# Three expert slots taken from the count before the last two chunks, and multiplied behind the last chunk's routing

## The chip, the cores and the metric

The kernel runs on one core of a Trainium2 chip. The metric is the device time of one execution in microseconds (us); the time of a kernel is the median of its timed runs. The engines are TensorE (PE, with its weight loads as PEld), VectorE (DVE), ScalarE (ACT), GpSimd (POOL) and SyncE (SP), whose work here is to issue DMAs.

## The reference, cut to what matters

The whole computation is four layers over 3125 nodes of 256 values: an attention layer, a mixture of 16 experts with two experts for each node, a graph sum, and a mixture of 8 experts with one expert for each node. Only the last layer is touched by the change:

```python
def _L1_ffn_ref(x, W1, b1, Wg, bg, Wd, bd):          # C = 256, HID = 1024, E = 8
    H = gelu(x @ W1 + b1)
    probs = softmax(H @ Wg + bg)
    assign = argmax(probs)
    out = zeros_like(x)
    for e in range(8):
        y = H @ Wd[e] + bd[e]
        out = out + where(assign == e, probs[:, e:e + 1] * y, 0)
    return out
x = x + _L1_ffn_ref(_layernorm(x), ...)
```

Each node goes through a common hidden layer of 1024 values, picks one of 8 experts by the gate, and is multiplied with that expert's 1024 x 256 weights. The result is weighted by the gate's probability and added to the node's x.

## The kernel before, in words

The last layer is the function `routed_top1`. It works in two phases.

**Routing.** The nodes come in 25 tiles of 128, and these in chunks of four tiles (512 nodes): six full chunks and a seventh with one tile, of which 53 nodes are real. A loop over the chunks (line 895 on) does this for each:

- PE computes the hidden layer `H` in eight parts (line 901) and ACT applies the Gelu (line 903).
- PE multiplies `H` with the gate's weights (line 910, `ps_zT`). DVE takes the result out as `zs` (line 912). PE folds it into logits (line 915), and DVE finds each node's expert (`first_max`, lines 240 to 248, and `sel`, line 921).
- `pre` (line 924) adds up `sel` tile by tile. Two small products on PE (lines 925 and 926) make of `sel` and `pre` each node's rank among the nodes of its expert, and DVE turns this into `to`, the node's row in a buffer in HBM called `rows` (line 933). Each expert has its own area of `rows`, filled without gaps from its start.
- ACT computes the Exp for the probability (line 936). Exp and Gelu need different tables, which ACT loads in between.
- For each tile, PE transposes `H` back (line 945, `ps_rows`), ACT or DVE copies it into `row` (line 946), POOL copies x in beside it (line 947), and DVE adds the node's number and probability (lines 948 and 949). POOL then issues an indirect DMA that scatters the 128 rows of 1282 values into `rows` (line 950).

**Slots.** A slot is one full or partly filled tile of 128 rows of one expert. Behind the last chunk, PE sums the number of nodes of each expert (`ps_n`, line 956), and DVE computes from it a table of slots: for each the expert and the first row (lines 959 to 987). While that goes on, `keep_warm` (line 555) lets PE multiply zeros. Then 30 slots run (`slots`, line 1007 on). For each:

- SP reads expert and row from the table (lines 1009 and 1011), loads the 128 rows into `hs` (line 1015), and loads the expert's bias (line 1017). The first slot's load is split in two. The pool of `hs` has four buffers. Since `rows` is written by scatters with addresses known only at run time, a load waits for all scatters ahead of it.
- PE transposes the tile (line 1022, `ps_cols`) and ACT copies it into `hsT` (line 1023).
- PE multiplies it with the expert's weights, which stay in SBUF (line 995, `ps_y`). DVE adds the bias (line 998), computes the weighted sum `y` (line 999), and casts the nodes' numbers to `who` (line 1002). POOL scatters `y` to the output (line 1003). The multiplication of a slot is issued behind the transposes of the next.

Two more slots (30 and 31) stand behind a branch that is taken only if the table has more than 30 (`rest`, line 969).

A scheduler of the language orders the instructions of each engine and puts in the waits. It takes both from the tiles that instructions read and write, and from the memory that a tile takes over when a pool is closed and the next one opened. The pools of the routing phase (`uh` for H, `ur` for rows, and others) are closed before the pools of the slots (`vx` for `hs`, `bias` and `hsT`, and others) are opened.

Of the kernel before, what the change touches and what calls it, by code (L numbers as in the profile page):

```python
# [9 lines left out]
F32 = mybir.dt.float32  # L10
F16 = mybir.dt.float16
BF16 = mybir.dt.bfloat16
I32 = mybir.dt.int32
# [3 lines left out]
OP = mybir.AluOpType  # L17
AX = mybir.AxisListType
# [3 lines left out]
P = 128  # L22
N = 3125
NT = 25
LAST = N - (NT - 1) * P
NP = NT * P
D = 256
# [10 lines left out]
NX1, HID1 = 8, 1024  # L38
EPS = 1e-5
CHUNK = 512  # L40
# [484 lines left out]
SLOTS = (N + NX1 * (P - 1)) // P  # L525
USUAL = 30
ROW0 = D + 2
ROW1 = HID1 + D + 2
# [23 lines left out]
def keep_warm(nc, ps, held, rows, times):  # L552

    for _ in range(times):
        nc.tensor.matmul(ps, held, rows, start=True, stop=True)


def independent(tc, group, made):

    tc.declare_no_dep(made.ins, group=group, reason="rows of different tokens")  # L560
    tc.add_to_no_dep_group(group, made.ins)
# [295 lines left out]
def routed_top1(tc, x, xnT, ident, iota, count, weights, rows, out, over):  # L857
# [4 lines left out]

    nc = tc.nc
    before, every = count
    (a, b1, (g, fold), gb), (d, bd) = weights
    nh = HID1 // P
    with tc.tile_pool(name="u1", bufs=1) as cp:
# [9 lines left out]
                                channel_multiplier=-1)  # L877
# [6 lines left out]
        warm = cp.tile([P, P], F32, name="warm")  # L884
        nc.gpsimd.memset(warm, 0.0)
        rest = cp.tile([1, 1], I32, name="rest")
        end = cp.tile([1, 4, 2 * NX1], F32, name="end")
        nc.vector.memset(end, 0.0)
        with tc.tile_pool(name="uh", bufs=2) as hp, tc.tile_pool(name="uw", bufs=2) as wp, \
             tc.tile_pool(name="ur", bufs=6) as rp, \  # L890
# [4 lines left out]
            for c in range(0, NP, CHUNK):  # L895
                n = min(CHUNK, NP - c)
                H = hp.tile([P, nh, CHUNK], F32, name="H")
# [55 lines left out]


            total = pg.tile([1, NX1], F32, name="ps_n")
            nc.tensor.matmul(total, every[:, 0:1], pre[:, NT], start=True, stop=True)
            nc.scalar.copy(warm[0:1, :NX1], total)
            keep_warm(nc, tp.tile([P, CHUNK], F32, name="ps_rows"), warm, d[:, 0, 0:2].rearrange("p j f -> p (j f)"), 8)
# [4 lines left out]

            nc.vector.tensor_copy(end[:, 0, NX1:], ni)
            for j in range(3):
                nc.vector.tensor_tensor(end[:, j + 1, NX1:], end[:, j, NX1:], end[:, j, NX1 - (1 << j):-(1 << j)],
                                        op=OP.add)
            end = end[:, 3, NX1:]
            nc.vector.tensor_scalar(rest, end[:, NX1 - 1:], float(USUAL), None, op0=OP.is_gt)
            slot = cp.tile([1, SLOTS], F32, name="slot")  # L970
            nc.gpsimd.iota(slot, pattern=[[1, SLOTS]], base=0, channel_multiplier=0,
                           allow_small_or_imprecise_dtypes=True)
            done = cp.tile([1, SLOTS, NX1], F32, name="done")
            nc.vector.tensor_tensor(done, end[:, None, :].to_broadcast([1, SLOTS, NX1]),
                                    slot[:, :, None].to_broadcast([1, SLOTS, NX1]), op=OP.is_le)
            ex = cp.tile([1, SLOTS], F32, name="ex")
            nc.vector.tensor_reduce(ex, done, AX.X, OP.add)
            nc.vector.tensor_scalar(table[:, 0], ex, float(NX1 - 1), None, op0=OP.min)

            nc.vector.tensor_tensor(done, done, ni[:, None, :].to_broadcast([1, SLOTS, NX1]), op=OP.mult)  # L980
            skip = cp.tile([1, SLOTS], F32, name="skip")
            nc.vector.tensor_reduce(skip, done, AX.X, OP.add)
            nc.vector.tensor_tensor(slot, slot, skip, op=OP.subtract)
            nc.vector.tensor_scalar(ex, ex, float(NT), None, op0=OP.mult)
            nc.vector.tensor_tensor(slot, slot, ex, op=OP.add)

            nc.vector.tensor_scalar(table[:, 1], slot, float(NX1 * NT), float(P), op0=OP.min, op1=OP.mult)

        def slots(which, pools):
            xp, sp, tp, po = pools  # L990

            def multiply(hs, hsT, bias, e):
                ps = po.tile([P, D], F32, name="ps_y")
                for j in range(nh):
                    nc.tensor.matmul(ps, hsT[:, j], d[:, ds(e, 1), j, :].rearrange("p o f -> p (o f)"),  # L995
                                     start=(j == 0), stop=(j == nh - 1))
                y = sp.tile([P, D], F32, name="y")
                nc.vector.tensor_tensor(bias, ps, bias, op=OP.add)  # L998
                nc.vector.scalar_tensor_tensor(y, bias, hs[:, HID1 + D + 1:], hs[:, HID1:HID1 + D], op0=OP.mult,  # L999
                                               op1=OP.add)  # L1000
                who = sp.tile([P, 1], I32, name="who")
                nc.vector.tensor_copy(who, hs[:, HID1 + D:HID1 + D + 1])  # L1002
                independent(tc, "out", nc.gpsimd.indirect_dma_start(  # L1003
                    out=out, out_offset=bass.IndirectOffsetOnAxis(ap=who, axis=0), in_=y, in_offset=None,
                    bounds_check=N - 1, oob_is_err=False))

            ready = None
            for s in which:
                e = nc.values_load(table[0:1, 0, s:s + 1], engines=(mybir.EngineType.PE, mybir.EngineType.SP), min_val=0,  # L1009
                                   max_val=NX1 - 1, skip_runtime_bounds_check_because="min with the last expert")  # L1010
                at = nc.values_load(table[0:1, 1, s:s + 1], engines=(mybir.EngineType.SP,), min_val=0,  # L1011
                                    max_val=NX1 * NP, skip_runtime_bounds_check_because="min with the spare tile")
                hs = xp.tile([P, ROW1], F32, name="hs")
                for c, n in ((0, ROW1),) if s else ((0, HID1 // 2), (HID1 // 2, ROW1 - HID1 // 2)):
                    nc.sync.dma_start(hs[:, c:c + n], rows[ds(at, P), c:c + n])  # L1015
                bias = xp.tile([P, D], F32, name="bias")
                nc.sync.dma_start(bias, bd[ds(e, 1), :].to_broadcast([P, D]))  # L1017
                hsT = xp.tile([P, nh, P], F32, name="hsT")
                for h in range(0, nh, 4):
                    ps = tp.tile([P, 4, P], F32, name="ps_cols")  # L1020
                    for j in range(4):
                        nc.tensor.transpose(ps[:, j], hs[:, (h + j) * P:(h + j + 1) * P], ident)  # L1022
                    nc.scalar.copy(hsT[:, h:h + 4], ps)  # L1023
                if ready:
                    multiply(*ready)
                ready = hs, hsT, bias, e
            multiply(*ready)

        def pools(stack, bufs):
            return [stack.enter_context(tc.tile_pool(name=name, bufs=b, **kw)) for name, b, kw in (  # L1030
                ("vx", min(4, bufs), {}), ("vs", bufs, {}), ("vpt", min(4, bufs), dict(space=PSUM)),
                ("vpo", min(3, bufs), dict(space=PSUM)))]

        with ExitStack() as stack:
            slots(range(USUAL), pools(stack, 6))
# [719 lines left out]
```

## Time and profile before

| | |
|---|---|
| Time of the kernel (median of 3 runs) | 1934.22 us (1934.16 to 1934.34) |
| The profiled execution: its own time | 1933.04 us |
| The profiled execution: span from first to last instruction | 1931.3 us |
| Mean granted PE clock | 0.991 of full |
| PE busy, DVE busy, ACT busy, POOL busy | 97%, 52%, 39%, 15% of the span |
| ps_y multiplications of the slots (line 995) | 480, 108.8 us busy |
| ps_H multiplications of the routing (line 901) | 224, 93.1 us busy |
| Last full chunk's zs copied out (line 912) | at 1766.37 us |
| Last chunk's scatter of rows issued (line 950) | at 1782.96 us |
| First load of a slot issued (line 1015) | at 1786.94 us |
| First transposes of a slot (line 1022) | at 1791.57 us |

Times within the profile are microseconds from the start of the span. An fp32 multiplication is recorded as two passes, so that eight products of a slot count as 16. Matmuls are pipelined, so two groups that follow one another may overlap a little in the records. The granted clock is the share of full speed that the chip allowed PE in a stretch of time.

### The profile page before, as it was taken

The numbers are of one execution on the slowest core, as the hardware profiler recorded it, in microseconds if no ns is written. First come the engines' busy times: TensorE is split into PE (matmuls) and PEld (weight loads), VectorE is DVE, ScalarE is ACT, GpSimd is POOL, SyncE is SP. The second block draws the span as 40 slices with busy tenths as digits, with TensorE's granted clock in tenths as the row PEclk, the third lists the DMA queues.
The fourth block names the chain that finished last, engine by engine and source line by source line (L and its number), as shares of the span: only waits on it lengthen the run. The fifth ranks groups of instructions, "written<-read, shape, count | busy, mean of one in ns | idle before, by whom it ended". The sixth has DMA issues, their size and how long they took to land. (4 is left out here: it accounts for less than half of the span.)

```text
span 1931.3 us, 27975 instructions
## 1 busy us (share of the span) xinstructions
PE 1867.0 (97%) x9466; PEld 1482.0 (77%) x9466; DVE 1002.7 (52%) x2909; ACT 748.3 (39%) x2254; POOL 297.2 (15%) x454
## 2 busy tenths in 40 slices
PE   6999999999999999999999989999989999999998
PEld 4788888887788888788888757777668887455887
DVE  6889888785555555567777722222235222334122
ACT  4767777672000011122222221111127999544221
POOL 4200000000000000022333222233320000132122
PEclk9999999999999999999999989999999999999999
DMA  4101123475100000021111165657540000633664
GB/s 124 32 10 64 40 67 121 198 288 231 68 1 1 1 1 3 9 56 45 44 45 44 39 201 145 193 175 235 128 107 2 1 1 1 229 137 143 214 209 138
DMA packets 103577, 182.96 MB, mean 95 GB/s; under 512 B 10054, under 2 KB 72741, under 8 KB 103392
## 3 DMA queue, kind: packets, MB, share of 16 engines
q1 hardware_dynamic: 72268, 124.32, 18.9%
q0 software_dynamic: 16016, 34.28, 6.5%
q10 hardware_dynamic: 15138, 22.44, 3.6%
q8 instruction: 80, 1.31, 0.3%
q14 instruction: 75, 0.61, 0.1%
HBM read 92.93 MB, written 90.17 MB: 95 GB/s over the span
## 5 line engine op out<-in xcount | busy, mean ns | idle before, releaser
L1263 PE MATMUL acc<-big,pm 128*128 128x257 f32 (+1 forms) x3750 | 872.1, 383 | 5.2 <-DVE pm L1260 4.8
L1263 PEld LDWEIGHTS acc<-big,pm 128*128 128x128 f32 (+1 forms) x3750 | 681.3, 187 | 111.4 <-DVE pm L1260 10.3
L1260 DVE SCALAR_TENSOR_TENSOR pm<-tau,rho,counts 128x256 f32<-128x256 f32 (+1 forms) x975 | 437.0, 467 | 160.3 <-PE acc L1263 157.5
L762 PE MATMUL ps_h<-xsT,w 128*128 128x384 f32 x512 | 167.8, 486 | 0.5 <-ACT xsT L738 0.5
L1382 PE MATMUL acc<-msg,cr 128*128 128x512 f32 (+1 forms) x625 | 157.9, 403 | 0.0
L1594 DVE TENSOR_TENSOR ohk<-iota_k,key 128x1200 f16<-128x1200 f16 x196 | 151.7, 775 | 5.7 <-PE acc_c L1606 5.4
L762 PEld LDWEIGHTS ps_h<-xsT,w 128*128 128x128 f32 x512 | 97.2, 190 | 65.1 <-ACT xsT L738 0.7
L1382 PEld LDWEIGHTS acc<-msg,cr 128*128 128x128 f32 (+1 forms) x625 | 114.7, 185 | 29.2 <-ACT cr L1378 1.2
L1378 ACT ACTIVATE cr<-counts 128x256 fp32r<-128x256 uint8 (+1 forms) x325 | 130.5, 402 | 14.6 <-PE acc L1382 7.0
L1606 PE MATMUL acc_c<-ohk,ohs 128*128 128x200 f16 x1176 | 130.6, 250 | 0.6 <-ACT ohs L1591 0.6
L1590 ACT ACTIVATE far<-iota_s,low 128x128 f16<-128x128 f16 x360 | 123.4, 397 | 6.1 <-POOL far L1588 1.8
L1606 PEld LDWEIGHTS <-ohs 128*128 128x128 f16 x1176 | 105.3, 98 | 25.9 <-ACT ohs L1591 1.0
L995 PE MATMUL ps_y<-t_wd,hsT 128*128 x480 | 108.8, 380 | 0.4 <-ACT hsT L1023 0.4
L765 ACT ACTIVATE silu<-ps_h 128x384 f32<-128x384 f32 x64 | 31.4, 490 | 199.6 <-PE ps_h L762 199.6
L766 DVE TENSOR_TENSOR hid<-silu,ps_h 128x384 f32<-128x384 f32 x64 | 35.5, 554 | 136.9 <-PE ps_h L762 134.5
L1609 ACT CAST counts<-acc_c 128x400 uint8<-128x400 f32 x196 | 93.0, 479 | 34.7 <-PE acc_c L1606 34.0
L995 PEld LDWEIGHTS ps_y<-t_wd,hsT 128*128 128x128 f32 x480 | 88.8, 190 | 11.6 <-ACT hsT L1023 0.6
L1243 ACT ACTIVATE tau<-ps_m 128x256 f32<-128x256 f32 (+1 forms) x39 | 14.1, 369 | 215.5 <-PE ps_m L1241 197.3
L780 POOL DMA_INDIRECT sums<-y,who x48 | 74.9, 1561 | 128.1 <-DVE y L778 118.5
L901 PE MATMUL ps_H<-big,t_w 128*128 128x512 f32 (+1 forms) x224 | 93.1, 552 | 0.8 <-ACT H L903 0.5
L775 PE MATMUL ps_o<-w,hid 128*128 128x256 f32 x384 | 86.8, 379 | 0.0
L1594 DVE TENSOR_TENSOR ohs<-iota_s,low 128x512 f16<-128x512 f16 (+1 forms) x196 | 83.6, 427 | 0.0
(298 smaller groups left out, 1933.2 us busy)
## 6 DMA issues: line engine op xcount, KB each, us to landing
rows<-empty SPq DMA_DIRECT2D x16, 2564.0 KB, 15.1
w<-in_L_ffn_w_dram ACTq DMA_DIRECT2D x42, 512.0 KB, 7.6
hs<-rows SPq DMA_DIRECT2D x29, 641.0 KB, 4.2
w<-in_L_ffn_w_dram SPq DMA_DIRECT2D x30, 512.0 KB, 5.3
rows<-empty SPq DMA_DIRECT2D x16, 516.0 KB, 4.3
t_wd<-in_L_ffn_Wd_dram SPq DMA_DIRECT2D x8, 1024.0 KB, 12.5
xs<-rows SPq DMA_DIRECT2D x15, 387.0 KB, 5.5
bias<-in_L_ffn_bd_dram SPq DMA_DIRECT2D x30, 128.0 KB
```

Of the source, the lines that this page charges most:

```text
L762: nc.tensor.matmul(ps, w[:, k, j * P:(j + 1) * P], xsT[:, k], start=(k == 0), stop=(k == KD - 1))
L775: nc.tensor.matmul(ps, hid[:, j, q * P:(q + 1) * P], o[:, j], start=(j == 0), stop=(j == nh - 1))
L901: nc.tensor.matmul(ps[:, :n], a[:, k, j * P:(j + 1) * P], xnT[:, k, c:c + n], start=(k == 0), stop=(k == KD - 1))
L995: nc.tensor.matmul(ps, hsT[:, j], d[:, ds(e, 1), j, :].rearrange("p o f -> p (o f)"), start=(j == 0), stop=(j == nh - 1))
L1260: nc.vector.scalar_tensor_tensor(pm[:, :n], tau[:, :n], now.rho[:, s:s + 1], edges[:, s, :n], op0=OP.max, op1=OP.mult)
L1263: nc.tensor.matmul(acc[:r, j, :D + 1], pm[:, q:q + r], now.h[:, s], start=(s == 0), stop=(s == NT - 1))
L1378: nc.scalar.activation(cr[:, :n], edges[:, s, :n], AF.Copy, accum_out=seen[:, a * NT + s:a * NT + s + 1])
L1382: nc.tensor.matmul(acc[:r, j].rearrange("p h d -> p (h d)"), cr[:, q:q + r], msg[:, s].rearrange("p h d -> p (h d)"), start=(s == 0), stop ...
L1590: nc.scalar.activation(far[:, i], self.iota_s, AF.Abs, scale=-1.0, bias=self.low32[:, pair, i:i + 1])
L1594: nc.vector.tensor_tensor(to[:, i:].rearrange("p t (x u) -> p t x u", u=2), iota.rearrange("p (x u) -> p x u", u=2)[:, None].to_broadcast( ...
L1606: nc.tensor.matmul(acc[:, u], ohs[:, i], ohk[:, i], start=(t == 0), stop=(t == TW - 1))
L1609: nc.scalar.copy(to[:, :, d0 % PAIR:d0 % PAIR + 2 * WIN].rearrange("p s (u d) -> p u s d", u=2), acc.rearrange("p u (s d) -> p u s d", d=WIN))
```

## The change

Ahead of the sixth chunk (the last with four tiles) the kernel now counts the nodes of each expert in the first five chunks, 2560 nodes, and divides by 128, rounding down: these are the tiles that are already full. A function `listed`, made of the former table code, writes a table of `SOONER` = 3 slots of such tiles. SP loads their rows and biases there. The rows go into tiles of the pool `ur`, which has seven buffers in place of six. Behind the routing of the last chunk these three slots are transposed and multiplied, one after the other, with the routing phase's own pools: the transposed tile is put into a tile `H`, the sums into `ps_H`. `taken` remembers how many tiles of each expert are done. The table that follows the last chunk lists only what is left, and the later loop runs slots 3 to 29; the limit behind which the branch is taken falls by three as well. `keep_warm` is no longer called here, and the first load of the later loop is no longer split. `turn` and `multiply` are the former code of a slot, made into functions for both uses.

```diff
+SOONER = 3
...
-        warm = cp.tile([P, P], F32, name="warm")
-        nc.gpsimd.memset(warm, 0.0)
+        taken = cp.tile([1, NX1 + 1], F32, name="taken")
+        nc.vector.memset(taken, 0.0)
+        def listed(name, n, start, lo, hi):
+            to = hi - lo
+            end = cp.tile([1, 4, 2 * NX1], F32, name=name + "_end")
+            nc.vector.memset(end, 0.0)
+            nc.vector.tensor_copy(end[:, 0, NX1:], n)
+            for j in range(3):
+                nc.vector.tensor_tensor(end[:, j + 1, NX1:], end[:, j, NX1:], end[:, j, NX1 - (1 << j):-(1 << j)],
+                                        op=OP.add)
+            end = end[:, 3, NX1:]
+            slot = cp.tile([1, to], F32, name=name + "_slot")
+            nc.gpsimd.iota(slot, pattern=[[1, to]], base=0, channel_multiplier=0,
+                           allow_small_or_imprecise_dtypes=True)
+            done = cp.tile([1, to, NX1], F32, name=name + "_done")
+            nc.vector.tensor_tensor(done, end[:, None, :].to_broadcast([1, to, NX1]),
+                                    slot[:, :, None].to_broadcast([1, to, NX1]), op=OP.is_le)
+            ex = cp.tile([1, to], F32, name=name + "_ex")
+            nc.vector.tensor_reduce(ex, done, AX.X, OP.add)
+            nc.vector.tensor_scalar(table[:, 0, lo:hi], ex, float(NX1 - 1), None, op0=OP.min)
+            step = cp.tile([1, NX1], F32, name=name + "_step")
+            nc.vector.tensor_tensor(step, start[:, 1:], start[:, :NX1], op=OP.subtract)
+            nc.vector.tensor_tensor(step, step, n, op=OP.subtract)
+            nc.vector.tensor_tensor(done, done, step[:, None, :].to_broadcast([1, to, NX1]), op=OP.mult)
+            skip = cp.tile([1, to], F32, name=name + "_skip")
+            nc.vector.tensor_reduce(skip, done, AX.X, OP.add)
+            nc.vector.tensor_tensor(slot, slot, skip, op=OP.add)
+            nc.vector.scalar_tensor_tensor(slot, ex, float(NT), slot, op0=OP.mult, op1=OP.add)
+            nc.vector.tensor_tensor(slot, slot, start[:, 0:1].to_broadcast([1, to]), op=OP.add)
+            nc.vector.tensor_scalar(table[:, 1, lo:hi], slot, float(NX1 * NT), float(P), op0=OP.min, op1=OP.mult)
+            return end
...
+        def turn(tp, name, hs, hsT):
+            for h in range(0, nh, 4):
+                ps = tp.tile([P, 4, P], F32, name=name)
+                for j in range(4):
+                    nc.tensor.transpose(ps[:, j], hs[:, (h + j) * P:(h + j + 1) * P], ident)
+                nc.scalar.copy(hsT[:, h:h + 4], ps)
...
-             tc.tile_pool(name="ur", bufs=6) as rp, \
+             tc.tile_pool(name="ur", bufs=7) as rp, tc.tile_pool(name="uy", bufs=2) as yp, \
...
             for c in range(0, NP, CHUNK):
                 n = min(CHUNK, NP - c)
+                if c // CHUNK == (NP - 1) // CHUNK - 1:
+                    total = pg.tile([1, NX1], F32, name="ps_n")
+                    nc.tensor.matmul(total, every[:, 0:1], pre[:, c // P], start=True, stop=True)
+                    full = cp.tile([1, NX1], I32, name="full")
+                    nc.vector.tensor_copy(full, total)
+                    nc.vector.tensor_scalar(full, full, 7, None, op0=OP.arith_shift_right)
+                    up = listed("soon", full, taken, 0, SOONER)
+                    soon = []
+                    bias4 = cp.tile([P, SOONER, D], F32, name="bias4")
+                    for i in range(SOONER):
+                        e, at = place_of(i)
+                        hs = rp.tile([P, ROW1], F32, name="row")
+                        nc.sync.dma_start(hs, rows[ds(at, P)])
+                        nc.sync.dma_start(bias4[:, i], bd[ds(e, 1), :].to_broadcast([P, D]))
+                        soon.append((hs, bias4[:, i], e))
+                    nc.vector.tensor_tensor(taken[:, :NX1], full, up, op=OP.subtract)
+                    nc.vector.tensor_scalar(taken[:, :NX1], taken[:, :NX1], float(SOONER), 0.0, op0=OP.add, op1=OP.max)
+                    nc.vector.tensor_tensor(taken[:, :NX1], taken[:, :NX1], full, op=OP.min)
...
+            for i, (hs, bias, e) in enumerate(soon):
+                if i % 4 == 0:
+                    hT = hp.tile([P, nh, CHUNK], F32, name="H")
+                hsT = hT.rearrange("p j n -> p (j n)").rearrange("p (i j n) -> p i j n", i=4, n=P)[:, i % 4]
+                turn(tp, "ps_rows", hs, hsT)
+                ps = pp.tile([P, CHUNK], F32, name="ps_H")
+                multiply(ps[:, :D], yp, hs, hsT, bias, e)
             total = pg.tile([1, NX1], F32, name="ps_n")
             nc.tensor.matmul(total, every[:, 0:1], pre[:, NT], start=True, stop=True)
-            nc.scalar.copy(warm[0:1, :NX1], total)
-            keep_warm(nc, tp.tile([P, CHUNK], F32, name="ps_rows"), warm, d[:, 0, 0:2].rearrange("p j f -> p (j f)"), 8)
...
+            left = cp.tile([1, NX1], F32, name="left")
+            nc.vector.tensor_tensor(left, ni, taken[:, :NX1], op=OP.subtract)
+            up = listed("late", left, taken, SOONER, SLOTS)
+            nc.vector.tensor_scalar(rest, up[:, NX1 - 1:], float(USUAL - SOONER), None, op0=OP.is_gt)
...
-                for c, n in ((0, ROW1),) if s else ((0, HID1 // 2), (HID1 // 2, ROW1 - HID1 // 2)):
-                    nc.sync.dma_start(hs[:, c:c + n], rows[ds(at, P), c:c + n])
+                nc.sync.dma_start(hs, rows[ds(at, P)])
...
-            slots(range(USUAL), pools(stack, 6))
+            slots(range(SOONER, USUAL), pools(stack, 6))
```

## The prediction

> **What bounds the kernel now.** The page comes first, for who is busy over the whole span:
>
> ```profile
> PE 1867.0 (97%) x9466; PEld 1482.0 (77%) x9466; DVE 1002.7 (52%) x2909; ACT 748.3 (39%) x2254; POOL 297.2 (15%) x454
> ```
>
> TensorE (PE) is almost always busy, so a change pays only where PE waits or does work that nobody needs. The chain that ended last, read next, shows the stage of this change: the last scatter of rows, loads that follow one another, then slots of 0.87 us of transposes and 3.46 us of multiplications, 4.33 us each, back to back until the end.
>
> ```profile
> 1782.96 3.55 DMA rows<-row,to
> ...
> 1790.84 6.85 DMA hs<-rows
> 1797.68 0.14 issue
> 1797.82 1.06 PE ps_cols L1022 x8
> 1798.89 3.46 PE ps_y L995 x16
> ...
> 1885.47 3.47 PE ps_y L995 x16
> 1888.96 0.44 DVE bias L998
> 1889.42 0.44 DVE y L999
> ```
>
> So the end moves with two things: when the first slot's transposes start, and how many slots follow. PE's timeline shows what lies ahead of that start (start, duration, instruction, and in brackets the idle time before it and who ended it):
>
> ```profile
> 1780.56 0.17 PE L925 MATMUL ps_r<-sel,before 128*128 128x8 bf16 x1 [1.29 <-DVE sel L921]
> 1780.58 0.17 PE L926 MATMUL ps_r<-pre,every 128*128 128x8 bf16 x1
> 1780.76 0.17 PE L956 MATMUL ps_n<-pre,every 128*1 128x8 bf16 x1
> 1781.71 10.02 PE L555 MATMUL ps_rows<-t_wd,warm 128*128 128x512 f32 x16 [0.78 <-issue]
> 1791.57 1.04 PE L1022 MATMUL ps_cols<-ident,hs 128*128 128x128 f32 x8
> 1792.96 2.51 PE L995 MATMUL ps_y<-t_wd,hsT 128*128 x10 [0.36 <-ACT hsT L1023]
> ```
>
> The 10.02 us of line 555 are multiplications whose result nobody reads. Behind them the last scatter lands (1786.51) and the first slot is loaded. This is the room that the change fills with three slots. The windows show what else those multiplications did (the number ahead of the DMA share is PE's granted clock):
>
> ```profile
> 1440.00:1442.00 2.00, 0.09 (x1) 0.12 (x2) 1.97 (x11) 0.59 (x2) 0.00 (x0) 0.50 1.03 343
> 1442.00:1444.00 2.00, 1.88 (x5) 1.19 (x6) 2.00 (x10) 0.67 (x2) 0.00 (x0) 0.50 0.88 274
> 1446.00:1448.00 2.00, 2.00 (x10) 1.73 (x11) 2.00 (x9) 0.73 (x3) 0.00 (x0) 0.94 1.06 343
> ...
> 1780.00:1782.00 2.00, 0.65 (x4) 0.50 (x4) 1.66 (x13) 1.54 (x3) 0.00 (x0) 0.69 0.98 387
> 1784.00:1786.00 2.00, 2.00 (x3) 0.67 (x2) 1.47 (x7) 0.00 (x0) 0.00 (x0) 0.50 0.35 136
> 1786.00:1788.00 2.00, 2.00 (x4) 0.86 (x3) 0.00 (x0) 0.00 (x0) 0.00 (x0) 0.60 0.04 8
> ```
>
> Around 1781 the clock falls to a half and comes back at 1787.6 (0.60 is 1.6 us of a half and 0.4 of full), 5.9 us after PE was busy again. Line 1343, which PE reached after 5.63 us of waiting, ran at a half until 1446.2, 4.3 us after its start. The useless multiplications took the slow clock in the first case; in the second, real work did.
>
> **The change, part by part.** *Removed:* the 10.02 us of line 555, the split of the first load, and three slots behind the last load: 3 x 4.33 = 12.99 us off the end.
>
> *Added on the way.* The "soon" list is one PE product (0.17 us) and some 23 small VectorE (DVE) instructions of 0.13 to 0.41 us, put after the fifth chunk, where DVE is idle from 1754.8 to 1766.4: nothing. PE reads the table three times; such a read is 0.30 us, and 30 of them vanish in slots that run at exactly 4.33: nothing, at most 0.9 us. SyncE (SP) now issues three row loads and three bias loads; its queue holds nothing else then. The row loads wait for the fifth chunk's scatters, whose traffic ends in the window 1762 to 1763 (31 GB/s in it, none after). With 0.43 us from landing to issue, as at 1786.51 to 1786.94, 4.2 us for a load, and 1.65 between issues (1789.18 to 1790.84), they land at 1766.7, 1768.4 and 1770.0.
>
> Two queues stand behind these loads. POOL's scatters of the sixth chunk must wait until the rows are read: they go at 1775.09 today, 5 us of cover. DVE stands closer: in the built order (how the built program's instructions stand on each engine) the cast who of the first early slot sits ahead of the sixth chunk's zs, and DVE takes its instructions in order.
>
> ```profile
> 1766.37 0.69 DVE L912 COPY zs<-ps_zT 128x512 f32<-128x512 f32 x1 [11.55 <-PE ps_zT L910]
> 1791.32 0.15 DVE L1002 CAST who<-hs 128x1 int32<-128x1 f32 x1 [5.73 <-DMA hs<-rows]
> ```
>
> The first row shows zs ready at 1766.37, so it is 0.3 us late; the second shows such a cast waiting for a load. The built order also moves one row copy of 0.6 us (line 946) from ahead of the sixth chunk's expert choice to the middle of it. Together I count 0.9 us for everything up to the last expert choice; from none (loads at the shortest, 3.9) to 3.5 us (loads at the longest, 6.8).
>
> ```profile
> DMA to landing us min/median/max: 3.9/4.2/6.8
> ```
>
> *The three early slots.* Their copies on ScalarE (ACT) stand behind the last Exp (table load and Exp end at 1781.56 today) and a row copy of 0.6 us: 1781.56 + 0.9 + 0.6 = 1783.1, and 0.6 more for the copy itself gives a first multiplication at 1783.7. They are not interleaved: each transposes, waits for its copies and multiplies. From the first transposes to the first multiplication it is 1.39 us (1791.57 to 1792.96), so the last one ends at 1783.7 + 3.46 + 2 x (1.39 + 3.46) = 1796.9 on a full clock. That is 13.2 us of work where 10.8 us of room was.
>
> *The wait that the change adds.* In the built order SP's first late load waits for PE's last early multiplication and for DVE's last early y, because the late pool of tiles takes the memory of the pools that just closed; before, the youngest PE work in that wait was the rank product of line 925. Behind it stand all later loads, and for them all 27 slots. So the load, which was hidden behind line 555, now starts after the early slots: 0.95 us for bias and y, 0.43 to the issue, 4.2 to land, 0.1 to PE: 5.65 us in which PE has nothing. The late table is no part of it: three more small instructions bring it to about 1787.5, long before.
>
> *The clock.* Nothing keeps PE busy now in either gap. After the two cases above PE ran at a half for 4.3 and 5.9 us of resumed work, 5.1 in the mean, which loses 2.6 us. In the first gap 0.4 of it falls on waits for ACT; in the second 0.4 falls on waits for loads that today's first slots have too (0.36 ahead of line 995, 0.18 at 1797.82). I take 2.2 us for each, from 0 (no drop) to 3.
>
> [...]
>
> *The sum.* The first late transposes start at 1796.9 + 2.2 + 5.65 = 1804.75 in place of 1791.57: 13.18 us later. Span: 1931.3 + 13.18 - 12.99 + 2.2 = 1933.7. The profiled execution took 1933.04, 1.74 over its span: 1935.4 for its like. The median of the timed runs is 1.18 above it, so 2.4 us on 1934.22: **1936.6 us**. A measurement of this kernel can tell about 0.2%, 3.9 us, from no change; I forecast no change by that.
>
> **The rivals.** *The clock holds* in both gaps. For it: the three early slots are real work that starts at once. Against: both cases of the trace. Then 1934.22 + 2.4 - 4.4 = 1932.2, still within the bound.
>
> *The loads stop DVE* (slower). The early loads take 6.8 us instead of 4.2, as one did at 1790.84 with others in flight. Who then ends at 1769.3, zs is 2.9 us late and every later step with it: 2.6 more than in my sum, 1939.2; with both clock losses at 3 it is 1940.8. It decides from a landing after about 1768.2, where the total passes 3.9 us. Against it: no other traffic lies in 1763 to 1773.
>
> *The first late load does not wait* (faster), because its tiles miss the early slots' memory. Then it lands by 1793 and PE goes from slot to slot: 5.65 us of gap and 2.2 of clock leave the sum, 1928.8. The built order's waits speak against it.
>
> *The early slots are not taken off the late list*, and the branch behind 30 slots runs two more: 8.7 us, about 1945. Against: the late list subtracts what was taken, and the limit falls by three too.
>
> **How the numbers follow.** My sum has 56 in 100, of which 45 lie within 3.9 us and 11 above, if the 0.9 and the clock terms lie high together; the held clock 17, all within; the stopped DVE 20, 16 above and 4 within; the load that does not wait 6, all below; two more slots 1. So faster 0.06, the same 0.66, slower 0.28. The range goes from the held clock's 1932.2, taken to 1932.0, to most of the stopped DVE, 1940.0.
>
> **What would show it.** In the changed profile: line 555 gone from this stage; early transposes from about 1782 and a last early multiplication near 1799; the first late load issued just after the third early y; PE idle for some 5.7 us near 1800 with a window at 0.50 or close to it behind that; then 27 slots at 4.33. I am wrong if late loads are issued before 1795, if PE has no gap near 1800, or if the sixth chunk's zs is over 2 us later than 1766.37.

## The result and the profile after

| | before | after |
|---|---|---|
| Median of 8 runs each | 1932.54 us | 1939.66 us |
| Ratio | 1 | 1.0034, 95% interval 1.0025 to 1.0043 |
| The profiled execution: its own time, span | 1933.04, 1931.3 us | 1936.57, 1934.8 us |
| First late transposes to PE's end | 1791.57 to 1922.68: 131.11 us, 30 slots | 1804.47 to 1926.51: 122.04 us, 27 slots |

The changed kernel is slower by a third of a per cent: 6.6 us by the ratio; the two medians lie 7.1 us apart. The profiled execution after is the fastest of its eight; the others lie up to 6.5 us above it. So this profile shows the least of what the change costs, and a second one is read below.

The page says of PE what it said before, a busy engine, and 15 fewer matmuls:

```profile
PE 1861.2 (96%) x9451; PEld 1479.1 (76%) x9451; DVE 1005.5 (52%) x2935; ACT 748.7 (39%) x2252; POOL 296.7 (15%) x454
```

PE's timeline after, in the stage that was shown of before (start, duration, instruction, idle time ahead of it and who ended it):

```profile
1781.79 0.17 PE L1008 MATMUL ps_r<-sel,before 128*128 128x8 bf16 x1 [1.48 <-DVE sel L1004]
1782.71 1.54 PE L935 MATMUL ps_rows<-ident,row 128*128 128x128 f32 x8 [0.55 <-PE ps_n L1047]
...
1795.06 3.72 PE L940 MATMUL ps_H<-t_wd,H 128*128 x16 [0.24 <-ACT H L936]
1804.47 2.11 PE L935 MATMUL ps_cols<-ident,hs 128*128 128x128 f32 x8 [5.68 <-DMA hs<-rows]
```

The useless multiplications are gone, and the three early slots stand in their place (lines 935 and 940). They end at 1798.78. Then PE has nothing for 5.68 us, until the first late load lands. A line of DVE's timeline, one of SP's and one of SP's waits (total us, times, longest) show why: the load is issued at 1800.02, just behind the third early y (1799.28 to 1799.76), and y is what SP waited for.

```profile
1799.28 0.48 DVE L944 SCALAR_TENSOR_TENSOR y<-bias,row 128x256 f32<-128x256 f32 x1
```

```profile
1800.02 0.33 SPq L1063 DMA_DIRECT2D hs<-rows  x1
```

```profile
SPq L1063 <- DVE y L944: 11.6, 1, 11.6
```

The windows (busy time of PE, PEld, DVE, ACT and POOL with counts, granted clock, DMA share, GB/s) show the price of the two idle times: the first early multiplications and the first late slots run on half a clock, behind the second gap until 1810.7.

```profile
1784.00:1786.00 2.00, 2.00 (x7) 1.63 (x6) 1.83 (x9) 0.59 (x1) 1.14 (x1) 0.50 0.27 108
1804.00:1806.00 2.00, 1.53 (x7) 1.36 (x8) 0.15 (x1) 0.12 (x1) 0.00 (x0) 0.50 0.95 289
...
1810.00:1812.00 2.00, 2.00 (x9) 1.68 (x8) 0.15 (x1) 0.59 (x1) 0.00 (x0) 0.81 0.82 319
```

DVE's timeline around the sixth chunk holds what the prediction had only half:

```profile
1766.06 0.15 DVE L947 CAST who<-row 128x1 int32<-128x1 f32 x1 [8.89 <-DMA row<-rows]
1766.65 0.69 DVE L995 COPY zs<-ps_zT 128x512 f32<-128x512 f32 x1 [0.36 <-PE ps_zT L993]
1769.60 0.15 DVE L947 CAST who<-row 128x1 int32<-128x1 f32 x1 [2.19 <-DMA row<-rows]
1769.67 0.18 DVE L1000 TENSOR_TENSOR z<-ps_z,t_bg 128x32 f32<-128x32 f32 x1
```

The first cast holds nothing up. It ends at 1766.21, and zs starts at 1766.65, when PE's product `ps_zT` is done. That is 0.28 us later than before because PE was already 0.28 us later; its timelines, before and after:

```profile
1764.33 1.92 PE L910 MATMUL ps_zT<-H,t_wg 128*32 128x512 f32 x16
```

```profile
1764.61 1.92 PE L993 MATMUL ps_zT<-H,t_wg 128*32 128x512 f32 x16
```

Over all profiles of the experiments zs starts anywhere from 1765.18 to 1767.62, and both ends of this range are kernels without early slots. The second cast stands between zs and the logits z and waits 2.19 us for its row load, which was issued at 1764.36. In the kernel before, z came 1.85 us after zs (the line below is from its DVE timeline); here it takes 3.02.

```profile
1768.22 0.19 DVE L917 TENSOR_TENSOR z<-ps_z,t_bg 128x32 f32<-128x32 f32 x1 [0.21 <-PE ps_z L915]
```

### The profile page after: what moved, and what is told of

It is laid out like the page before. It is cut to its first block, busy times and chain, and to the rows that moved or that the text cites. A ratio compares the mean times of both kernels' runs of the same rounds, so it can differ in the third digit from the quotient of the medians.

```text
span 1934.8 us, 27977 instructions
## 1 busy us (share of the span) xinstructions
PE 1861.2 (96%) x9451; PEld 1479.1 (76%) x9451; DVE 1005.5 (52%) x2935; ACT 748.7 (39%) x2252; POOL 296.7 (15%) x454
## 4 chain that ended last, share of the span: by engine, by line
PE 84%; issue 5%; DMA 4%; ACT 3%; DVE 2%; POOL 1%; SPq 0%; POOLq 0%; ACTq 0%; DVEq 0%
PE acc L1307 39%; PE ps_h L763 9%; PE acc L1426 7%; PE ps_o L776 4%; PE ps_H L984 4%; PE acc_c L1650 4%; PE ps_y L940 3%; PE ps_m L1155 3%; DMA out_dram<-y,who 2%; PE ps_h L808 1%; PE ps_m L1409 1%; PE acc L1429 1%; PE ps_rows L1028 1%; DMA hs<-rows 1%; PE ps_cols L935 1%
## 5 line engine op out<-in xcount | busy, mean ns | idle before, releaser
L940 PE MATMUL ps_y<-t_wd,hsT 128*128 x432 | 98.8, 382 | 0.0
L940 PEld LDWEIGHTS ps_y<-t_wd,hsT 128*128 128x128 f32 x432 | 80.6, 192 | 10.2 <-ACT hsT L936 0.3
```

## The experiments

The theories at the start were three, and they do not exclude one another. **The added wait:** the first late load waits for the last early y, 5.7 us of gap. **The cast in order:** who waits on DVE for loads, and what stands behind it on DVE waits too. **The clock:** each idle time of PE is followed by half speed. Ratios are to the kernel before. For the changed kernel there are two measurements, 1.0034 and 1.0029 (below); where a difference in us is given, it is to their middle, 1.0032, times 1933, and uncertain by some 2.2 us, from the two half-widths.

From the profile of each run come these times in us. The last column starts at the sixth chunk's zs and so leaves out what differs ahead of the change.

| run | zs to z, sixth chunk | zs to zs of the last chunk | PE idle ahead of the late slots | half clock around first gap, second gap | zs to the span's end |
|---|---|---|---|---|---|
| before | 1.85 | 12.00 | none | 6.8, none | 164.9 |
| after | 3.02 | 12.65 | 5.68 | 3.4, 6.8 | 168.2 |
| again | 3.89 | 14.59 | 5.57 | 3.4, 10.2 | 171.0 |
| who_late | 3.46 | 13.10 | 5.51 | 3.4, 10.2 | 169.1 |
| who_soon | 1.84 | 11.98 | 5.83 | 3.4, 6.8 | 166.1 |
| who_all | 1.84 | 11.99 | 5.27 | 3.4, 10.2 | 167.9 |
| warm | 3.27 | 12.90 | 0.34 (filled) | 3.4, none | 166.2 |
| own | 1.85 | 11.98 | 0.86 | 6.8, 3.4 | 164.0 |
| own_soon | 1.84 | 11.98 | 0.52 | none, none | 160.1 |
| one | 1.85 | 12.00 | 8.17 | none, 6.8 | 164.9 |
| warm_soon | 1.85 | 11.99 | 0.69 (filled) | 3.4, none | 164.6 |
| before_who | 1.84 | 12.00 | none | 3.4, none | 165.9 |
| before_cold_who | 1.84 | 11.99 | 8.97 | 10.2 in its one gap | 167.3 |
| two | 1.84 | 11.98 | 1.57 | 3.4, 3.4 | 160.2 |

### again: the changed kernel a second time

No edit.

> The changed kernel with nothing altered, to see a second profile of it. All theories: 1.0034 of the kernel before, as first measured. What tells them apart is the profile, since the first profile (1936.57 us) was the fastest of its eight runs and the others lay up to 6.5 us above it. If the cast who on DVE, which stands in the late loop between bias and y and waits for a load, makes up the difference (theory of the in-order cast), this profile shows more idle time of PE behind hs in the loop than the 0.77 and 0.21 us of the first one, and DVE waiting more than 34.9 us for hs. If the difference comes from the clock (theory of the clock), the windows at 0.50 behind the two gaps are longer than 3.4 and 6.8 us. If it is only from elsewhere in the program, the stage from the last chunk to the end looks as in the first profile.

1.0029 (1.0018 to 1.0040). Its profile is that of a typical run (1939.51 us; the median is 1939.24). Against the first profile three things are worse. DVE's and PE's timelines and a window of this run:

```profile
1770.62 0.15 DVE L947 CAST who<-row 128x1 int32<-128x1 f32 x1 [3.07 <-DMA row<-rows]
```

```profile
1772.69 0.33 PE L1028 MATMUL ps_rows<-ident,H 128*128 128x128 f32 x1 [1.66 <-DVE row L1029]
```

```profile
1774.00:1776.00 2.00, 2.00 (x11) 1.74 (x10) 1.57 (x7) 0.37 (x1) 0.00 (x0) 0.50 0.03 8
1812.00:1814.00 2.00, 2.00 (x6) 1.59 (x5) 0.00 (x0) 0.00 (x0) 0.00 (x0) 0.50 0.24 91
```

The second cast waits 3.07 us. DVE's copies of the sixth chunk come late, PE waits 1.66 us for one of them, and the clock falls in the middle of the chunk's work (0.50 at 1774 to 1776; 1.00 there in the first profile). The last chunk's zs is 14.59 us behind the sixth's, 2.6 more than before. Behind the second gap the half clock lasts until 1814.0 in place of 1810.7. Stalls at hs in the late loop from 1860 on add up to 1.55 us (0.98 in the first profile), and DVE waits 38.8 us for hs with its casts (34.9). So the spread comes from the cast, from the clock, and a little from the late loop.

### who_late, who_soon, who_all: the cast on another engine

```diff
-            nc.vector.tensor_copy(who, hs[:, HID1 + D:HID1 + D + 1])
+            (nc.gpsimd if sp is not yp else nc.vector).tensor_copy(who, hs[:, HID1 + D:HID1 + D + 1])   # who_late: the late loop
+            (nc.gpsimd if sp is yp else nc.vector).tensor_copy(who, hs[:, HID1 + D:HID1 + D + 1])       # who_soon: the early slots
+            nc.gpsimd.tensor_copy(who, hs[:, HID1 + D:HID1 + D + 1])                                    # who_all
```

> In the late loop alone the cast who goes to POOL, so that DVE has only bias and y there. Theory of the in-order cast: the loads are again freed at the pace of PE, SP issues one every 4.33 us in place of about 5, the stalls of PE of about 1 us at slots 13 and 14 go, and with them whatever more the other runs had: 1 to 3 us faster than the changed kernel, 1.002 to 1.003 of the kernel before, and a smaller spread between runs. Theory of the added wait and the clock alone: the gap of 5.7 us and the slow stretch behind it stay and the late loop was hardly stalled: within 0.5 us of the changed kernel, 1.0034.

1.0027 (1.0017 to 1.0037). In the built order of the changed kernel's late loop, the cast of a slot three ahead stands between bias and y of the present one. Its y frees the buffer of the next load, so the loads space out: SP issued them 4.5 to 5.5 us apart between 1832 and 1867, where before has 4.33, and so has who_late but for one of 4.66. The view of waits shows it in the changed kernel (total us, times, longest):

```profile
DVE who L947 <- DMA hs<-rows: 34.9, 18, 4.7
```

In who_late that pattern and the stalls from 1820 on are gone. But the time fell by only 1.0 us or so, within the uncertainty. The coupling shows in the loads' times; a price of it can't be measured.

> Only for the three early slots the cast who goes to POOL, out of the way of the sixth chunk's zs and z on DVE. Theory that these casts delay the last chunk: z comes 1.45 us and the last expert choice about 1.2 us earlier, and so does everything behind it: 1.2 us faster than the changed kernel, 1.0028 of the kernel before; who on POOL ahead of the scatters of the sixth chunk costs nothing, since these go 5 us later. Theory that the delay is absorbed by a wait for the Exp table on ACT or by the scatters: the early slots start as before, no change, 1.0034.

1.0011 (1.0002 to 1.0020): 4.1 us better than the changed kernel, more than I expected. Its DVE has z where before has it, 1.84 us behind zs:

```profile
1769.25 0.19 DVE L1000 TENSOR_TENSOR z<-ps_z,t_bg 128x32 f32<-128x32 f32 x1 [0.21 <-PE ps_z L998]
```

The profiles show 1.3 to 2.1 us of it: from zs to the end of the last early multiplication it is 30.8 us, against 32.1, 32.5 and 32.9 in after, again and who_late. Where the rest comes from isn't shown; the clock that falls inside the sixth chunk, as in again, may be a part, and not every profile has it.

> Both at once: who is cast on POOL everywhere. If both parts of the theory of the in-order cast hold, their gains add up, 2 to 4 us: 1.0013 to 1.0024 of the kernel before. If only the added wait of the late load and the clock count, 1.0034 as the changed kernel. Slower than the changed kernel only if a cast of 128 elements on POOL holds up a scatter behind it so long that y's buffers run out, of which nothing in the profile speaks.

1.0010 (1.0001 to 1.0019), as who_soon alone. The early casts are a price of the change, the late ones are not one that can be measured.

### warm: the second gap filled with work that nobody reads

```diff
                 multiply(ps[:, :D], yp, hs, hsT, bias, e)
+            keep_warm(nc, pp.tile([P, CHUNK], F32, name="ps_H"), d[:, 0, 0, :P], d[:, 0, 0:2].rearrange("p j f -> p (j f)"), 6)
```

> The changed kernel with six more multiplications of 128x512 whose result nobody reads, behind the third early slot; they read only the weights, so that the first late load doesn't wait for them. At full clock one takes 0.865 us (twice the 0.43 of a 128x256 one), six 5.2 us, so that of the second gap (5.5 to 5.8 us) some 0.5 us are left. Theory that half the price of the late load's wait is the slow clock behind it: no slow window behind 1800, where four profiles of the changed order had 6.8 or 10.2 us of it; 3 to 5 us faster than the changed kernel, 1.0008 to 1.0018 of the kernel before, and a smaller spread. Theory that the chip slows its clock there for another reason (the change of load between two kinds of work): the slow windows stay, 1.0029 to 1.0034.

1.0006 (0.9997 to 1.0015): 5.0 us better. The added multiplications read only weights, so the late load goes as early as without them. PE's timeline and a window of this run:

```profile
1800.00 5.31 PE L556 MATMUL ps_H<-t_wd 128*128 128x512 f32 x12
1805.65 1.24 PE L935 MATMUL ps_cols<-ident,hs 128*128 128x128 f32 x8 [0.34 <-DMA hs<-rows]
```

```profile
1804.00:1806.00 2.00, 1.66 (x6) 0.45 (x4) 0.15 (x1) 0.00 (x0) 0.00 (x0) 1.00 0.71 241
```

The late transposes start 5.5 us after the last early multiplication, as in the changed kernel. What differs is the clock: every window from 1788 to 1818 is at 1.00. The change to other work is the same here, so the slow clock of the changed kernel goes with the idle time and not with that change, and by this run it costs about as much as the gap itself; in the five profiles that have it, it is 6.8 to 10.2 us of half speed, of which PE was busy for 5.5 to 8.5, so that 2.7 to 4.2 us are lost.

### own, own_soon: a buffer that the routing never held

```diff
+        held = ExitStack()
+        ox = held.enter_context(tc.tile_pool(name="ox", bufs=1))     # opened ahead of the routing's pools
...
-                hs = xp.tile([P, ROW1], F32, name="hs")
+                own = s == SOONER
+                hs = (ox if own else xp).tile([P, ROW1], F32, name="hs")
...
+                if own:
+                    multiply(*ready)
+                    ready = None
+            if ready:
+                multiply(*ready)
```

To make room, zs moves to a pool with one buffer, and `uy` has one in place of two. own_soon has the edit of who_soon as well.

> The changed kernel with a buffer of its own for the first late slot (slot 3), which no pool of the routing held, so that its load waits for scatters alone; it is multiplied at once, and the next loads wait for the last early y as before. Theory of the added wait: slot 3 runs in what was the gap, the gap shrinks from 5.6 to about 1 us in pieces, and no slow window follows: 5 + 3 to 5 = 8 to 10 us faster than the changed kernel less 0.5 for the slot that isn't interleaved: 0.999 to 1.0000 of the kernel before. Theory that the casts on DVE and the last chunk's delay are the main price: the gap goes but the clock still falls in the first one and the delay stays: 1.001. If the load lands late for another reason (the table): PE still waits some us near 1799, 1.003.

0.9985 (0.9976 to 0.9994): 9.1 us better than the changed kernel, and faster than the kernel before. But the edit did one thing more: in its built order the second early cast no longer stands ahead of z (1.85 us behind zs in the table). So the clean comparison is that of who_soon with own_soon, which has the cast on POOL too: 1.0011 to 0.9986, 4.8 us (uncertain by 2.5) for the added wait and what hangs on it.

> Both: slot 3 with its own buffer, and the cast who of the early slots on POOL. If the added wait and the casts in the way of the sixth chunk are two prices that add up: 2 to 3 us faster than with the own buffer alone, as it was without it (1.0011 against 1.0029 to 1.0034): 0.997 to 0.9985 of the kernel before, faster than both kernels. If the delay of the last chunk only moved the first slots into the same wait, no gain over the own buffer alone.

0.9986 (0.9977 to 0.9995). No further gain, since own had moved the cast already; the two gains were not there to add. SP issues the first late load at 1788.05, behind the table (ready at 1787.51) and ahead of two of the three early y, so the wait is gone for this load. A line of SP's timeline, then PE's with what is left of the gap:

```profile
1788.05 0.33 SPq L1067 DMA_DIRECT2D hs<-rows  x1
```

```profile
1796.42 1.10 PE L935 MATMUL ps_cols<-ident,hs 128*128 128x128 f32 x8 [0.52 <-DVE bias L942]
1797.92 3.72 PE L940 MATMUL ps_y<-t_wd,hsT 128*128 x16 [0.41 <-ACT hsT L936]
1803.06 1.09 PE L935 MATMUL ps_cols<-ident,hs 128*128 128x128 f32 x8 [1.42 <-DMA hs<-rows]
...
1806.82 1.07 PE L935 MATMUL ps_cols<-ident,hs 128*128 128x128 f32 x8 [1.30 <-DMA hs<-rows]
```

Slot 3 fills the flight of the next load but for 1.42 us, and no slow window follows.

### one: a single early slot

```diff
-SOONER = 3
+SOONER = 1
```

> SOONER is 1 in place of 3: one early slot, 29 late ones. By the sum of the prediction an early slot costs 4.85 us (1.39 + 3.46, not interleaved) and saves 4.33, so two fewer are worth 1.0 us; the gap of 5.6 us and its slow clock stay; and there is only one cast who on DVE, in front of zs and not of z, so the 1.2 to 2 us of z's delay go too: 2 to 3 us faster than the changed kernel, 1.0015 to 1.002. If the three slots themselves bring the gain that the prediction counted (12.99 us off the end against 13.2 added) and the fixed prices are smaller than thought, it is as the changed kernel or slower, 1.003 to 1.005.

1.0004 (0.9995 to 1.0013): 5.4 us better than the changed kernel, with two early slots fewer. The late transposes start at 1794.92, 9.55 us earlier than after, and two more late slots cost 8.66, which leaves 0.9 us. That this is near the 1.0 expected is chance, for three things went into it that the 1.0 left out. The cast ahead of z is gone, which who_soon puts at 4.1. The early multiplication ran at full clock. And the gap is longer, 8.17 us, because y of the one early slot goes ahead of the late table on DVE and the table is ready only at 1789.6. The slow clock began at 1791.3, inside the gap, so only 3.1 us of it fell on work (the transposes at 1794.92 took 1.94 us, those at 1798.29 1.10).

### warm_soon: both cures without the buffer

The edits of warm and who_soon together.

> The six useless multiplications behind the third early slot and the cast who of the early slots on POOL, together; the gap behind the early slots (the late load's wait) stays. Theory of three prices that add up (casts in the way of the last chunk, slow clock behind the second gap, the gap itself): alone they gave 1.0011 and 1.0006 of the kernel before, against 1.0029 to 1.0034 with neither, so together 0.9982 to 0.9990, with the gap of 5.6 us still there, filled by work that nobody reads. Rival: the slow clock costs less when the last chunk isn't delayed, or the reverse, so that the two gains are partly the same one: 1.000 to 1.0006.

0.9995 (0.9984 to 1.0006). If the gains added up fully it would be 0.9985. The interval holds that and the rival's whole range (1.000 to 1.0006) as well, so additivity isn't decided by it. Its profile (164.6 us from zs to the end) is 1.6 better than warm's, with the same 3.4 us of half clock.

### before_who and before_cold_who: the useless multiplications alone

Both have who on POOL; the second has no line 555 as well:

```diff
-            nc.scalar.copy(warm[0:1, :NX1], total)
-            keep_warm(nc, tp.tile([P, CHUNK], F32, name="ps_rows"), warm, d[:, 0, 0:2].rearrange("p j f -> p (j f)"), 8)
```

> The kernel before with the cast who on POOL, a control for the next run. There the casts of the late loop stand behind y for most slots, and no slot was late: all theories say no change, 0.999 to 1.001.

> The same without the ten us of multiplications that nobody reads (line 555), one part of the change done alone: PE waits some 10 us for the first slot's load. Theory of the clock: the slow clock of the first gap, which those multiplications took, now falls on the first slots; 6.8 to 10.2 us of it less what falls into the gap: 3 to 4 us slower than the control, 1.0015 to 1.002 of it. By the prediction's term it is 2.2 to 3 us. Rival: the clock recovers while PE waits, as it does not need work to come back: the same as the control, 1.000.

0.9994 (0.9984 to 1.0003) and 1.0008 (0.9997 to 1.0019): 2.7 us between them, with an uncertainty of 2.8, so the size is open. The profile shows the mechanism (PE's timeline, then a window):

```profile
1788.70 2.01 PE L1020 MATMUL ps_cols<-ident,hs 128*128 128x128 f32 x8 [8.97 <-DMA hs<-rows]
```

```profile
1786.00:1788.00 2.00, 0.00 (x0) 0.00 (x0) 0.00 (x0) 0.00 (x0) 0.00 (x0) 0.50 0.61 150
```

PE waits at half speed and starts its slots at half speed: the clock fell at 1782.6, and no window from 1784 to 1792 is above 0.50. So here the clock did not come back in the last 6.1 us of PE's wait.

### two: two early slots, and two buffers of their own

The edits of own_soon with other sizes: `ur` has six buffers again, and the second of the two slots with own buffers is multiplied at once.

```diff
-SOONER = 3
+SOONER = 2
...
+        ox = held.enter_context(tc.tile_pool(name="ox", bufs=2))
+                own = s < SOONER + 2
+                bias = (ox if own else xp).tile([P, D], F32, name="bias")
+            y = bias if sp is yp else sp.tile([P, D], F32, name="y")
```

> Two early slots and the next two slots in buffers of their own, rows and bias, whose loads wait for scatters alone; the third and later ones wait for the last early y as before. The cast who of the early slots is on POOL, and the early y is written over the bias. Theory of the added wait: slots 2 and 3 now cover the whole flight of the load of slot 4, so the pieces of some 1.4 and 1.3 us in which PE still waited for hs with one buffer go (2.7 us), and one early slot fewer is worth 0.5: 2 to 3 us faster than with one buffer of its own (0.9986), 0.9970 to 0.9977 of the kernel before. Rival: PE is by then held by something else (the copies of ACT, or the loads that follow one another on 16 queues): as with one buffer, 0.9982 to 0.9990.

0.9951 (0.9935 to 0.9967): 9.5 us faster than the kernel before and 16 us faster than the changed one. One wait of some size is left ahead of the late slots, for the load that the table (ready at 1789.95) now releases:

```profile
1795.08 1.06 PE L935 MATMUL ps_cols<-ident,hs 128*128 128x128 f32 x8 [1.57 <-DMA hs<-rows]
```

The gain over own_soon, 0.0035, is more than the 2 to 3 us expected, and the profiles don't show it: from zs to the end both have 160.1 or 160.2 us. The profiled execution of two is the slowest of its six runs, that of own_soon the fastest of its eleven. So it is shown that two beats both kernels, but not how much it is worth over one buffer.

## Why the prediction was right, and where it was not

The forecast of 1936.6 us lies within 0.2% of the median measured, 1939.66, which is inside the range. Some of this closeness is luck: the median of before that I started from, 1934.22, is 1.7 us above that of its eight runs. Of the change itself I forecast 2.4 us, and it is 6.6. And the likeliest case, no change that a measurement can tell, didn't come: the kernel is slower by 0.34%, the side that had the second chance.

**Right: the order of things and the gap.** The early multiplications were to end near 1799 (1798.78), the first late load to follow the third early y (0.26 us behind it), the gap to be 5.65 us (5.68), the late transposes to start at 1804.75 (1804.47). The run that took this wait away for one load (own_soon, against who_soon) gained 4.8 us. The clock fell behind both gaps of the first profile.

**Mis-sized, and put in the wrong place: the 0.9 us up to the last expert choice.** I had found the cast ahead of zs, and gave it 0.3; it cost nothing. Its load landed 3.6 us after its issue, quicker than the 4.2 I took. The same built order has the second cast ahead of z, and I didn't follow it down to there. I let the second load land at 1768.4, 4.0 us after its issue (1764.36). Its cast was free to go only at 1769.6, 5.2 us after it, and in again at 1770.6. The last expert choice (`sel`) comes 14.9, 16.6, 15.4 and 15.6 us after the sixth chunk's zs in the four profiles with this cast (after, again, who_late, warm), against 14.0 before: 1.0 to 2.7 us. So the first profile has about the 0.9 forecast, from another cast than I thought. Over whole runs, who_soon puts all that hangs on the casts at 4.1 (1.9 to 6.3) us. That is the rival in which the loads stop DVE, with its price about right and its place wrong: I would have looked for it at zs, 2 us late, and zs was not.

**Mis-sized: the clock of the second gap.** I took 2.2 us, at most 3, from two cases with 4.3 and 5.9 us of half speed after work resumed. Here PE was busy at half speed for 6.1 us in the first profile and 8.5 in again, half of which is lost: 3.0 and 4.2. The first late slots then waited for loads once more (0.21 us in the first profile, 0.64 in again), and half speed lasted for 6.8 and 10.2 us. The run warm gives 5.0 (2.8 to 7.2). The first gap cost 1.6 in the first profile (2.2 predicted): on a full clock the prediction's steps from the first multiplication at 1784.04 end at 1797.2, not 1798.78. In before_cold_who, the kernel before with PE idle in its one gap, it was 4.0 us of resumed work.

**Left out: the late loop.** It was to run at 4.33 us a slot. From the first transposes to the end it gained 131.11 - 122.04 = 9.07 us, where 12.99 less 2.2 for the clock were counted. Of the 3.9 us between 9.07 and 12.99 the clock took 3.0, the rest are stalls for loads. Freed of its casts, the loop gains nothing that can be measured.

**Mis-judged: the step from profile to median.** I added 1.18 us, what three runs of before showed; its eight runs have their median 0.5 us below the profile. The changed kernel's median lies 3.1 us above its profile. A reason that fits, though no run tests it alone: before has one stretch of half speed in this stage, and useless work stands in it; the change has two in each of its two profiles, with real work in both.

With what the runs gave for the two mis-sized terms, 4.1 for 0.9 and 5.0 for 2.2, the sum of 2.4 becomes 8.4 us, against 6.6 measured: within what the two runs leave uncertain, and they may overlap, since part of the first may be clock too.

## What to carry to other kernels

In the changed kernel the first load into memory that closed pools had held was issued 0.26 us behind the last y of the work that used them; into a buffer that the routing's pools had never held (own_soon) it was issued at 1788.05, ahead of two of the three early y. When work is moved into the shadow of a load, see first whether the load now waits for the moved work; with the cast out of the way as well, a buffer of its own for the first tile, never held by the phase before, took this change from 0.1% slower to 0.15% faster, and two of them, with one early slot fewer, to 0.5% faster.

The second cast is 0.15 us of work. It waited 2.19 us for its row load (3.07 in again), and z, which stands behind it on DVE, came 3.02 us behind zs (3.89) in place of 1.85. A small instruction that reads a freshly loaded tile was such a wait here. Follow every such instruction through the built order, not only the first, and put it on an engine that has nothing due.

The gap of PE of 5.3 to 5.8 us cost twice in the five profiles that have it unfilled: its own length, and 6.8 or 10.2 us of half speed, of which PE was busy for 5.5 to 8.5. Price both.

## What the runs showed of the hardware

In the thirteen profiles that have half speed in this stage, a stretch of it lasts 3.4, 6.8 or 10.2 us: one, two or three pieces of 3.41 (the first one of the profile after goes from 1783.45 to 1786.86). In six of the profiles with two of them the second starts 13.7 us behind the first (two), 17.1 (who_late), 20.5 (after, who_soon, who_all) or 30.7 (again), each time a whole number of 3.41. Eight transposes took 1.04 us at full clock and 2.07 at a half (after, at 1788.96 and 1807.95). So where work fills the whole of such a piece, it costs 1.7 us, an estimate from these two figures.

The clock fell behind short idle times too. In before it fell at 1780.7 with 1.29 us of idle time of PE in the 3.41 us ahead, and in again at 1773.1 with 1.79. But idle time alone does not decide: in own_soon PE had the same pause of 1.29 us, ahead of 1780.51, and every window from 1770 to 1818 is at 1.00. And among the slots the clock stayed with 1.71 us in the 3.41 ahead (after, at 1800.5) and fell with 1.81 (own, at 1808.8). What else it takes, no run tests.

For the return the profiles show this: in all these stretches the clock came back after the first piece in which PE was idle for at most 0.39 us (who_all, at 1785.3), and never after one with 0.46 (who_late, at 1809.3) or more. The same gap of 5.3 to 5.8 us was followed by two pieces in after and who_soon and by three in again, who_late and who_all. In the second piece, PE was idle for 0.21 us and not at all in the first two, and for 0.63, 0.46 and 1.15 us in the other three, with waits of the first late slots for their loads in it. That the return hangs on this idle time is a reading of these profiles; no run tests it alone.
